# Squares of the keys issued a group later on ScalarE, and the keys' transposes in a PSUM bank of their own

## The chip, the cores and the metric

The kernel runs on one core of a Trainium2 chip. The metric is the device time of one execution in microseconds (us), the median of the runs. Everything is in float32. Five engines work beside each other, each through its own instructions in order: TensorE (PE, with its weight loads as PEld), VectorE (DVE), ScalarE (ACT), GpSimd (POOL) and SyncE (SP), which here issues DMAs.

## The reference

Two layers run one after the other on eight sequences of 100 tokens (512 wide), with a context of 722 rows for each sequence. The first layer aligns tokens to context rows by dynamic time warping, sums for each token the context rows that are matched to it into the tokens, and then runs a mixture of 16 experts in which each token goes to three. The second layer is a cross-attention with normalised queries and keys, and a feed-forward part. What the change touches are the keys and values of that second cross-attention:

```python
xn = layernorm(x, ln_x_g, ln_x_b)            # x: the context rows
ln = layernorm(latents, ln_l_g, ln_l_b)      # latents: the tokens
q = ln @ W_q
kv = jnp.concatenate([xn @ W_kv, ln @ W_kv], axis=1)
k, v = (kv[..., :INNER], kv[..., INNER:])
...
qn = rmsnorm(q, q_gamma) * SCALE
kn = rmsnorm(k, k_gamma)                     # n = norm(k) / sqrt(64); k / max(n, 1e-8) * gamma, for each head
sim = jnp.einsum('bhid,bhjd->bhij', qn, kn)
```

The context's part of keys and values depends on nothing that the first layer computes, so it can be done at any time before the attention.

## The kernel before

The kernel is one program whose instruction order on each engine is fixed when it is built, by a scheduler that goes by priorities and by its own estimates of durations. So work of different stages stands interleaved in each queue, and since every engine takes its queue in order, an instruction that has to wait holds up everything behind it, of whatever stage.

The stages around the change, with the lines of the profile:

- *Alignment* (codes L369 to L376, wave L392 to L395, traceback L440 with one step a token): almost all on VectorE. It ends at 402.80 us, with the copy `sel` (L448) behind it.
- *Keys and values of the context*, called the key stage here (L678 to L769): runs beside the alignment on PE, ScalarE and GpSimd, and reaches on into all stages down to the first expert slot. It is the code that the change edits.
- *Sums*: path values are spread over partitions by PE (`pf`, L453), copied by ScalarE (`fb`, L458), turned into selections by VectorE (`below` and `on`, L469 and L470), multiplied with the context rows `cr` (DMAs L476 and L479) by PE (`pe`, L483), copied (`er`, L485), moved by DMA to `E` (L490), and added to the tokens X by VectorE (L494).
- *Routing*: normalised tokens `xh`, transposed on PE (`pt`, L550) and multiplied with the gate (`pl`, L554, its logits `g` read at L558); then softmax, ranks (`pw`, L571) and places on VectorE; `pg`/`gT` (L668, L669) and `po` (L673, added to X at L674) bring in the experts' second bias; 21 indirect DMAs on GpSimd put the tokens into their experts' rows (`xs_d`, L645).
- *Expert slots* (`slot`, L778): SP fetches an expert's weights `w1t`, `w2t`, its bias `b1t` and its rows `xr` (L785 to L792); PE transposes the rows (`px`, L796), VectorE copies them (`xe`, L798); then PE computes `ph` (L807) and `py` (L822). Weights of odd slots lie in a pool, `moewb`, that takes the memory which the key stage used, so they are fetched when the key stage's last use of it has ended.
- Then the attention, which reads keys and values back from the DRAM tensors `k_d` and `v_d`, and the feed-forward part.

The key stage handles 16 groups: for each of eight sequences, two groups of three chunks of 128 context rows. `products` does a group's matmuls and copies; `keys` normalises and transposes the keys of a group, and is called one group behind. In `products`, each chunk has two PSUM tiles, `pk` and `pv`, of four matmuls each (L720); ScalarE copies the key tile with its row scale (`k`, L724), GpSimd adds the bias (L725), ScalarE copies the value tile (`vr`, L726); after the three chunks GpSimd issues the values' DMAs to `v_d` (L728, L733). Then ScalarE takes the squares of each chunk and head (8 heads, so 24 a group, L737, with the sum into `rk`), and the root (L740). In `keys` VectorE takes maximum and reciprocal of `rk` (L746, L747), GpSimd multiplies the keys with it chunk by chunk (L750), PE transposes each chunk in four pieces (`ptk`, L754), ScalarE copies these out (`kt`, L755), and GpSimd issues the DMA to `k_d` (L757).

All PSUM tiles of the key stage share one pool with one tag, so `pk`, `pv` and `ptk` take turns in four banks. In SBUF `k`, `vr` and `rk` have two buffers each, and `kt` and the scratch `kjunk` one.

Of the kernel before, what the change touches and what calls it, by code (L numbers as in the profile page):

```python
# [1 line left out]

# [7 lines left out]
F32 = mybir.dt.float32  # L10
U8 = mybir.dt.uint8
I32 = mybir.dt.int32
AF = mybir.ActivationFunctionType
# [4 lines left out]
P = 128  # L18
B, S, D = 8, 100, 512
# [11 lines left out]
NH, DH = 8, 64  # L31
# [38 lines left out]
def kernel(  # L70
# [25 lines left out]
    nc = tc.nc  # L96
# [98 lines left out]
    def ranks(sc, ne, pool):  # L195

        tri = pool.tile([P, ne, ne], F32, tag="tri", name="tri")
        nc.gpsimd.memset(tri, 1.0)
        nc.gpsimd.affine_select(
            out=tri, in_=tri, compare_op=ALU.is_gt, fill=0.0, base=0,  # L200
            pattern=[[1, ne], [-1, ne]], channel_multiplier=0,
        )
        other = sc.unsqueeze(2).to_broadcast([P, NT, ne, ne])
        own = sc.unsqueeze(3).to_broadcast([P, NT, ne, ne])
        ahead = pool.tile([P, NT, ne, ne], F32, tag="ahead", name="ahead")
        same = pool.tile([P, NT, ne, ne], F32, tag="same", name="same")
        nc.vector.tensor_tensor(ahead, other, own, ALU.is_gt)
        nc.vector.tensor_tensor(same, other, own, ALU.is_equal)
        nc.vector.tensor_tensor(same, same, tri.unsqueeze(1).to_broadcast([P, NT, ne, ne]), ALU.mult)
        nc.vector.tensor_tensor(ahead, ahead, same, ALU.add)  # L210
        rank = pool.tile([P, NT, ne], F32, tag="rank", name="rank")
        nc.vector.tensor_reduce(rank, ahead, AX.X, ALU.add)
        return rank, tri
# [27 lines left out]
    with tc.tile_pool(name="dwork", bufs=2, side="right") as dw, tc.tile_pool(name="dpsum", bufs=6, space=PSUM) as dps:  # L241
# [9 lines left out]
        pb = dps.tile([P, D], F32, tag="mm", name="pb")  # L251
# [16 lines left out]
        for b in range(B):  # L268
# [25 lines left out]
            r0, c0 = LAG + b * LANES, (B - 1 - b) * GW  # L294
# [30 lines left out]
    kvp = kv_scope.enter_context(tc.tile_pool(name="kv", bufs=2, side="right"))  # L325
    kps = kv_scope.enter_context(tc.tile_pool(name="kvpsum", bufs=4, space=PSUM, side="right"))
# [5 lines left out]
    with tc.tile_pool(name="align", bufs=2) as al:  # L332
# [77 lines left out]
        k, i = 1, 0  # L410
        while k < LANES:
            nc.vector.stream_shuffle(moved[:, body], last[:, i, LEAD - k : LEAD - k + NSTEP], over(k))
            nc.vector.tensor_tensor(last[:, 1 - i, body], last[:, i, body], moved[:, body], ALU.max)
            k, i = 2 * k, 1 - i
# [15 lines left out]
        for j in range(S - 1, -1, -1):  # L430
# [8 lines left out]
            junk = al.tile([B, W], F32, tag="junk", name="junk", bufs=1)  # L439
# [6 lines left out]
    with tc.tile_pool(name="sums", bufs=2) as sp, tc.tile_pool(name="spsum", bufs=4, space=PSUM) as sps:  # L446
# [4 lines left out]
        for b in range(B):  # L451
            k = b % half
# [49 lines left out]
    if True:  # L502
# [176 lines left out]
        mean = kvw.tile([P, P], F32, name="mean")  # L679
        nc.gpsimd.memset(mean, 1.0 / D)  # L680
        for half, dst in ((0, kbias), (1, vbias)):
            pb = kps.tile([P, D], F32, tag="mm", name="kvb")
            for dc in range(DC):
                nc.tensor.matmul(
                    pb, lncol[:, 1, dc : dc + 1].to_broadcast([P, P]), wc[:, dc, half * D : (half + 1) * D],
                    start=dc == 0, stop=dc == DC - 1,
                )
            nc.scalar.copy(dst, pb)
        pb = kps.tile([P, D], F32, tag="mm", name="kvc")
        for vc in range(DC):  # L690
            for dc in range(DC):
                nc.tensor.matmul(
# [5 lines left out]
            nc.scalar.mul(wc[:, dc, :], wc[:, dc, :], lncol[:, 0, dc : dc + 1])  # L698
        cm = kvw.tile([P, 2 * D], F32, name="cm")
        for half in range(2):  # L700
            pb = kps.tile([P, D], F32, tag="mm", name="kvm")
            for dc in range(DC):
                nc.tensor.matmul(
                    pb, mean, wc[:, dc, half * D : (half + 1) * D], start=dc == 0, stop=dc == DC - 1
                )
            nc.scalar.copy(cm[:, half * D : (half + 1) * D], pb)
        for dc in range(DC):
            nc.gpsimd.tensor_tensor(wc[:, dc, :], wc[:, dc, :], cm, ALU.subtract)
        def products(b, ct, c0):

            k = kvp.tile([P, 3, D], F32, tag="k", name="k")
            vr = kvp.tile([P, 3, D], F32, tag="vr", name="vr")
            rk = kvp.tile([P, 3, NH], F32, tag="rk", name="rk")
            for c in range(c0, c0 + 3):
                rs = crstd[:, b, c : c + 1]
                pk = kps.tile([P, D], F32, tag="mm", name="pk")
                pv = kps.tile([P, D], F32, tag="mm", name="pv")
                for ps, lo in ((pk, 0), (pv, D)):
                    for dc in range(DC):
                        nc.tensor.matmul(  # L720
                            ps, ct[:, dc, c * P : (c + 1) * P], wc[:, dc, lo : lo + D], start=dc == 0, stop=dc == DC - 1
                        )
                kc = k[:, c - c0, :]
                nc.scalar.mul(kc, pk, rs)  # L724
                nc.gpsimd.tensor_tensor(kc, kc, kbias, ALU.add)  # L725
                nc.scalar.mul(vr[:, c - c0, :], pv, rs)  # L726
            full = 3 if c0 == 0 else 2
            nc.gpsimd.dma_start(  # L728
                out=v_d[b, c0 * P : (c0 + full) * P, :].rearrange("(c p) d -> p c d", p=P), in_=vr[:, :full, :]
            )  # L730
            if c0 > 0:
                for r0, r1 in ((0, RLAST // 16 * 16), (RLAST // 16 * 16, RLAST)):
                    nc.gpsimd.dma_start(out=v_d[b, (RC - 1) * P + r0 : (RC - 1) * P + r1, :], in_=vr[r0:r1, 2, :])  # L733
            junk = kvp.tile([P, DH], F32, tag="kjunk", name="kjunk", bufs=1)
            for c in range(3):
                for h in range(NH):
                    nc.scalar.activation(  # L737
                        junk, k[:, c, h * DH : (h + 1) * DH], AF.Square, accum_out=rk[:, c, h : h + 1]
                    )
            nc.scalar.activation(rk, rk, AF.Sqrt, scale=1.0 / DH)  # L740
            return b, c0, k, rk

        def keys(b, c0, k, rk):

            kt = kvp.tile([P, NPAIR, 3 * P], F32, tag="kt", name="kt", bufs=1)
            nc.vector.tensor_scalar_max(rk, rk, 1e-8)  # L746
            nc.vector.reciprocal(rk, rk)  # L747
            for c in range(3):
                kh = k[:, c, :].rearrange("p (h d) -> p h d", h=NH)
                nc.gpsimd.tensor_tensor(kh, kh, rk[:, c, :].unsqueeze(2).to_broadcast([P, NH, DH]), ALU.mult)  # L750
                ptk = kps.tile([P, D], F32, tag="mm", name="ptk")
                ptv = ptk.rearrange("p (c n) -> p c n", c=NPAIR)
                for hp in range(NPAIR):
                    nc.tensor.transpose(ptv[:, hp, :], k[:, c, hp * P : (hp + 1) * P], ident)  # L754
                nc.scalar.activation(kt[:, :, c * P : (c + 1) * P], ptv, AF.Copy, scale=gcol[:, 1:2])  # L755
            w = min(S2 - c0 * P, 3 * P)
            nc.gpsimd.dma_start(out=k_d[b, :, :, c0 * P : c0 * P + w], in_=kt[:, :, :w])  # L757

        behind = None
        for b in range(B):  # L760
            ct = kvp.tile([P, DC, RC * P], F32, tag="ctk", name="ctk")
            nc.gpsimd.memset(ct[:, :, S2:], 0.0)
            nc.gpsimd.dma_start(out=ct[:, :, :S2], in_=context_t[b].rearrange("(c p) i -> p c i", p=P))
            for c0 in range(0, RC, 3):
                now = products(b, ct, c0)
                if behind is not None:
                    keys(*behind)
                behind = now
        keys(*behind)  # L769

        slots = moe.enter_context(ExitStack())
# [84 lines left out]
        with tc.If(some > 0):  # L856
            with tc.tile_pool(name="spw", bufs=1) as mw, tc.tile_pool(name="sph", bufs=2) as mh, tc.tile_pool(
                name="sppsum", bufs=4, space=PSUM
# [35 lines left out]
    if True:  # L894
# [8 lines left out]
        if True:  # L903
# [63 lines left out]
            with tc.tile_pool(name="qkv", bufs=2, side="right") as qp:  # L967
# [5 lines left out]
                for t in range(NT):  # L973
# [64 lines left out]
                    while r0 < t * P + n:  # L1038
                        b = r0 // S
# [6 lines left out]
                    while given < B and (given + 1) * S <= t * P + n:  # L1046
                        pv = aps.tile([P, D], F32, tag="po", name="apv", bufs=1)
# [5 lines left out]
                        vr = qp.tile([S, D], F32, tag="avr", name="avr")  # L1053
# [128 lines left out]
            def project(t):  # L1182
                n = tok_rows(t)
                py = aps.tile([P, D], F32, tag="tr", name="py", bufs=1)
                for dc in range(DC):
                    nc.tensor.matmul(  # L1186
                        py[:n], oT[:, dc, t * P : t * P + n], wo[:, dc, :], start=dc == 0, stop=dc == DC - 1
                    )
                return py
# [7 lines left out]
            done, ets, behind = 0, {}, None  # L1197
# [3 lines left out]
            with hand:  # L1201
                for g in range(B * NPAIR):
                    b, hp = g // NPAIR, g % NPAIR
# [8 lines left out]
                    if behind is not None and hp == 3:  # L1212
                        added(*behind)
                        behind = None
# [49 lines left out]
    with tc.tile_pool(name="ffn", bufs=1) as fp, tc.tile_pool(name="ffnt", bufs=3) as ft, tc.tile_pool(  # L1264
        name="fpsum", bufs=2, space=PSUM
# [48 lines left out]
        rank, _ = ranks(w, FE, fp)  # L1314
# [181 lines left out]
```

## Time and profile before

| | |
|---|---|
| median of the runs | 1538.27 us (three runs, 1536.83 to 1538.72) |
| the profiled execution | 1538.33 us |
| span of its trace | 1536.6 us |
| mean granted clock of TensorE | 0.949 |
| PE busy | 1385.6 us, 90% of the span |
| matmuls of pk and pv (L720) | 191.9 and 176.1 us |
| squares on ScalarE (L737) | 98.0 us, and 72.0 us of reading their sums |
| PE idle ahead of pk | 25.8 us, of which 22.7 for ScalarE's copy of vr |

Lines of the profile name the source line, the engine, the operation and its tiles (output<-inputs). Behind a bar stand busy time and the mean duration of one in ns, then the idle time of that engine just before such instructions, and what ended it. Waits are told as "engine, tile and line <- what it waited for: us in all, times, longest". The timeline shows start, duration and, in brackets, the idle time before. A clock of 0.50 in a window means that TensorE was granted half of its clock.

Some places of the trace that the prediction refers to: the sums' `pf` starts at 411.60 us; `pe` of the last sequence ends at 487.8; routing's last logits (`pl`) end at 529.5; the 21 puts lie between 561.63 and 588.3; the last `po` is at 608.30; the first slot's `px` starts at 613.63 and its `ph` at 616.88; the second slot's `ph` starts at 649.13.

### The profile page before, as it was taken

The page shows a single profiled execution, that of the slowest core. Times are in us where ns is not written, and L with a number is a line of the kernel's source. Part 1 is how long each engine was busy: PE and PEld are TensorE (multiplying, and loading weights), DVE is VectorE, ACT ScalarE, POOL GpSimd, SP SyncE. Part 2 cuts the span into 40 slices and gives each one's busy share as a digit, 9 for nine tenths or more (in the row PEclk, how much of TensorE's full clock was granted, in tenths as well). Part 3 has the DMA queues.
Part 4 walks back from the last instruction along what each step waited for, and adds up shares of the span by engine and source line. Part 5 has one row for each costly group of instructions (what it writes and reads, how often), then busy time and mean ns, then how long its engine had stood idle before and what let it go on. Part 6 is the DMA issues. An engine that isn't in the chain of part 4 may idle for free. (4 is left out here: it accounts for less than half of the span.)

```text
span 1536.6 us, 19541 instructions
## 1 busy us (share of the span) xinstructions
PE 1385.6 (90%) x7043; PEld 870.6 (57%) x7043; DVE 684.9 (45%) x1492; ACT 485.2 (32%) x1506; POOL 436.1 (28%) x552
## 2 busy tenths in 40 slices
PE   5979887989799998999999996499999997899998
PEld 4443333444333543899999995144476765544433
DVE  3579999799723251101100100634477773322220
ACT  3424354554522554121122221132354543200000
POOL 1014333545423356000000000600365554322210
PEclk8989899999999998899999998699899999999999
DMA  9861213542655143866567786521544420400000
GB/s 307 298 169 38 78 51 109 167 122 71 207 169 158 56 163 139 291 245 237 204 228 250 260 291 237 143 48 35 194 139 133 134 89 1 164 0 0 1 23 21
DMA packets 120857, 217.78 MB, mean 142 GB/s; under 512 B 47765, under 2 KB 49077, under 8 KB 120629
## 3 DMA queue, kind: packets, MB, share of 16 engines
q1 hardware_dynamic: 103413, 152.54, 30.9%
q0 software_dynamic: 16464, 61.44, 11.5%
q10 hardware_dynamic: 880, 2.51, 0.5%
q8 instruction: 58, 0.95, 0.3%
q14 instruction: 42, 0.34, 0.1%
HBM read 163.92 MB, written 50.86 MB: 140 GB/s over the span
## 5 line engine op out<-in xcount | busy, mean ns | idle before, releaser
L720 PE MATMUL pk<-wc,ctk 128*128 128x512 f32 x384 | 191.9, 641 | 25.8 <-ACT vr L726 22.7
L720 PE MATMUL pv<-wc,ctk 128*128 128x512 f32 x384 | 176.1, 597 | 0.0
L807 PE MATMUL ph<-xe,w1t 128*128 128x192 f32 (+4 forms) x1024 | 171.5, 314 | 1.3 <-DVE xe L798 1.3
L822 PE MATMUL py<-hT,w2t 128*128 128x192 f32 (+4 forms) x1024 | 169.7, 310 | 0.0
L807 PEld LDWEIGHTS ph<-xe,w1t 128*128 128x128 f32 x1024 | 154.4, 192 | 4.7 <-DVE xe L798 1.7
L822 PEld LDWEIGHTS py<-hT,w2t 128*128 128x128 f32 x1024 | 153.1, 191 | 1.8
L720 PEld LDWEIGHTS pk<-wc,ctk 128*128 128x128 f32 x384 | 76.9, 205 | 123.6 <-issue 92.8
L737 ACT ACTIVATE kjunk<-k 128x64 f32<-128x64 f32 x384 | 98.0, 255 | 111.3 <-POOL k L725 95.5
L811 ACT ACTIVATE hT<-ph,b1t 128x192 f32<-128x192 f32 (+4 forms) x128 | 51.8, 404 | 253.4 <-PE ph L807 253.4
L720 PEld LDWEIGHTS pv<-wc,ctk 128*128 128x128 f32 x384 | 73.1, 191 | 91.6 <-issue 88.6
L1129 ACT ACTIVATE et<-et,mk 128x200 f32<-128x200 f32 (+2 forms) x224 | 85.8, 451 | 67.2 <-DVE et L1123 67.1
L725 POOL TENSOR_TENSOR k<-k,kbias 128x512 f32<-128x512 f32 x48 | 71.9, 1503 | 99.1 <-ACT k L724 98.9
L798 DVE COPY xe<-px 128x768 f32<-128x768 f32 (+4 forms) x16 | 14.0, 875 | 185.8 <-PE ph L807 170.4
L835 POOL DMA_DIRECT2D ys_d<-yr x28 | 15.3, 547 | 285.8 <-ACT yr L834 285.8
L1356 PE MATMUL fpb<-xT,wi 128*128 128x400 f32 x256 | 91.5, 507 | 1.0 <-DVE z L1378 1.0
L1405 PE MATMUL fpo<-wot,hw 128*128 128x512 f32 x192 | 84.8, 595 | 0.0
L750 POOL TENSOR_TENSOR k<-k,rk 128x512 f32<-128x512 f32 x48 | 63.7, 1353 | 60.2 <-DVE rk L747 60.2
L440 DVE SCALAR_TENSOR_TENSOR junk<-two_i,path,C 8x735 f32<-8x735 f32 x64 | 74.1, 1157 | 9.7 <-DMA C<-step_d 7.7
L1113 PE MATMUL pst<-qt,akt 64*128 64x100 f32 x896 | 66.3, 282 | 6.8 <-DVE et L1123 6.7
L737 ACT ACTIVATION_READ_ACCUMULATOR kjunk<-k 128x1 f32 x384 | 72.0, 188 | 0.0
L1356 PEld LDWEIGHTS fpb<-xT,wi 128*128 128x128 f32 x256 | 47.0, 190 | 42.5 <-issue 9.4
L943 DVE CUSTOM_DVE_ANT_0 junk<-psc,mb 100x822 f32<-100x822 f32 x64 | 64.2, 1003 | 13.6 <-PE psc L933 13.3
(334 smaller groups left out, 2031.3 us busy)
## 6 DMA issues: line engine op xcount, KB each, us to landing
w1t<-in_w SPq DMA_DIRECT2D x16, 2048.0 KB
w2t<-in_w SPq DMA_DIRECT2D x16, 2048.0 KB
ct<-in_context_t SPq DMA_DIRECT2D x8, 1444.0 KB
ctk<-in_context_t POOLq DMA_DIRECT2D x8, 1444.0 KB
akt<-k_d SPq DMA_DIRECT2D x8, 1444.0 KB
cr<-in_context SPq DMA_DIRECT2D x8, 1280.0 KB
va<-v_d SPq DMA_DIRECT2D x8, 1280.0 KB
v_d<-vr POOLq DMA_DIRECT2D x8, 768.0 KB
```

The costliest lines, as they stand in the source:

```text
L440: nc.vector.scalar_tensor_tensor(junk, two_i1, path[:, j + 1 : j + 2], scol, ALU.is_le, ALU.mult, accum_out=path[:, j : j + 1])
L720: nc.tensor.matmul(ps, ct[:, dc, c * P : (c + 1) * P], wc[:, dc, lo : lo + D], start=dc == 0, stop=dc == DC - 1)
L725: nc.gpsimd.tensor_tensor(kc, kc, kbias, ALU.add)
L737: nc.scalar.activation(junk, k[:, c, h * DH : (h + 1) * DH], AF.Square, accum_out=rk[:, c, h : h + 1])
L750: nc.gpsimd.tensor_tensor(kh, kh, rk[:, c, :].unsqueeze(2).to_broadcast([P, NH, DH]), ALU.mult)
L807: nc.tensor.matmul(ph[:, :cap], st["w1t"][:, dc, hc * P : (hc + 1) * P], st["xe"][:, dc, :cap], start=dc == 0, stop=dc == DC - 1,)
L822: nc.tensor.matmul(py[:, dc, :cap], st["w2t"][:, hc, (2 * dh + dc) * P : (2 * dh + dc + 1) * P], st["hT"][:, hc, :cap], start=hc == 0, sto ...
L943: nc.vector.tensor_tensor_reduce(out=junk, in0=ps.rearrange("p b c -> p (b c)")[:S, :KEYS], in1=st["mb"], scale=1.0, scalar=-FMAX, op0=ALU ...
L1113: nc.tensor.matmul(ps[:, i, (c - c0) * S : (c - c0 + 1) * S], st["kt"][rows, hp, STARTS[c] : STARTS[c] + KP], qt[rows, hp, b * S : (b + 1) ...
L1129: nc.scalar.activation(et[:n, c - c0], et[:n, c - c0], AF.Exp, bias=mk[:n, b, c : c + 1])
L1356: nc.tensor.matmul(pb[:, :N2], wi[fc * P // FQ][:, dc, fc * P % FQ : fc * P % FQ + P], xT[:, dc, hh * N2 : (hh + 1) * N2], start=dc == 0, ...
L1405: nc.tensor.matmul(po[:n], hw[:, fc, t * P : t * P + n], wot[:, fc, :], start=fc == 0, stop=fc == FC - 1)
```

## The change

It has three parts. The squares and the root move from `products` into `keys`, and the squares of each chunk are put on ScalarE's queue behind the value copy of the same chunk of the following group, by an ordering edge (`tc.issue_after`) that adds no semaphore; for the last group there is no following group, and no edge. The transposes' tile `ptk` gets a tag of its own with one PSUM bank, and `pk`, `pv` and the setup's tiles keep three of the four. And `k` gets three buffers in place of two.

```diff
-                pk = kps.tile([P, D], F32, tag="mm", name="pk")
-                pv = kps.tile([P, D], F32, tag="mm", name="pv")
+                pk = kps.tile([P, D], F32, tag="mm", name="pk", bufs=3)
+                pv = kps.tile([P, D], F32, tag="mm", name="pv", bufs=3)
...
-            k = kvp.tile([P, 3, D], F32, tag="k", name="k")
+            k = kvp.tile([P, 3, D], F32, tag="k", name="k", bufs=3)
             vr = kvp.tile([P, 3, D], F32, tag="vr", name="vr")
-            rk = kvp.tile([P, 3, NH], F32, tag="rk", name="rk")
+            out_of = []
...
-                nc.scalar.mul(vr[:, c - c0, :], pv, rs)
+                out_of.append(nc.scalar.mul(vr[:, c - c0, :], pv, rs))
...
+            return b, c0, k, out_of
+
+        def keys(b, c0, k, _, later=()):
+
+            rk = kvp.tile([P, 3, NH], F32, tag="rk", name="rk")
             junk = kvp.tile([P, DH], F32, tag="kjunk", name="kjunk", bufs=1)
             for c in range(3):
-                for h in range(NH):
-                    nc.scalar.activation(
-                        junk, k[:, c, h * DH : (h + 1) * DH], AF.Square, accum_out=rk[:, c, h : h + 1]
-                    )
+                with tc.issue_after(later[c].ins) if later else nullcontext():
+                    for h in range(NH):
+                        nc.scalar.activation(
+                            junk, k[:, c, h * DH : (h + 1) * DH], AF.Square, accum_out=rk[:, c, h : h + 1]
+                        )
             nc.scalar.activation(rk, rk, AF.Sqrt, scale=1.0 / DH)
-            return b, c0, k, rk
-
-        def keys(b, c0, k, rk):
-
             kt = kvp.tile([P, NPAIR, 3 * P], F32, tag="kt", name="kt", bufs=1)
...
-                ptk = kps.tile([P, D], F32, tag="mm", name="ptk")
+                ptk = kps.tile([P, D], F32, tag="tk", name="ptk", bufs=1)
...
                 if behind is not None:
-                    keys(*behind)
+                    keys(*behind, later=now[-1])
                 behind = now
         keys(*behind)
```

More of the change, by code (lines that the diff above doesn't have):

```diff
@@ L1 @@
-from contextlib import ExitStack
+from contextlib import ExitStack, nullcontext
 import concourse.bass as bass
@@ L681 @@
         for half, dst in ((0, kbias), (1, vbias)):
-            pb = kps.tile([P, D], F32, tag="mm", name="kvb")
+            pb = kps.tile([P, D], F32, tag="mm", name="kvb", bufs=3)
             for dc in range(DC):
@@ L688 @@
             nc.scalar.copy(dst, pb)
-        pb = kps.tile([P, D], F32, tag="mm", name="kvc")
+        pb = kps.tile([P, D], F32, tag="mm", name="kvc", bufs=3)
         for vc in range(DC):
@@ L700 @@
         for half in range(2):
-            pb = kps.tile([P, D], F32, tag="mm", name="kvm")
+            pb = kps.tile([P, D], F32, tag="mm", name="kvm", bufs=3)
             for dc in range(DC):
```

## The prediction

> **What bounds the kernel now.** I read the page first (busy shares, then the costliest groups), then the waits of 120 to 630 us, the table of windows over the same time, and last the timeline at the places that these named. Groups of the page (busy time, mean of one, then idle time before them and what ended it), and three lines of the waits:
>
> ```profile
> PE 1385.6 (90%) x7043; PEld 870.6 (57%) x7043; DVE 684.9 (45%) x1492; ACT 485.2 (32%) x1506; POOL 436.1 (28%) x552
> ...
> L720 PE MATMUL pk<-wc,ctk 128*128 128x512 f32 x384 | 191.9, 641 | 25.8 <-ACT vr L726 22.7
> L737 ACT ACTIVATE kjunk<-k 128x64 f32<-128x64 f32 x384 | 98.0, 255 | 111.3 <-POOL k L725 95.5
> ```
> ```profile
> ACT kjunk L737 <- POOL k L725: 95.5, 39, 11.9
> ...
> DVE rk L746 <- ACT rk L740: 32.1, 5, 16.3
> ...
> PE ptk L754 <- ACT vr L726: 8.8, 4, 4.5
> ```
>
> TensorE is the busy engine, and the change aims at the few places where it isn't: it waits for ScalarE's copy of values (vr), which frees a PSUM bank. The timeline shows why that copy is late:
>
> ```profile
> 205.94 0.26 ACT L737 ACTIVATE kjunk<-k 128x64 f32<-128x64 f32 x1
> ...
> 206.57 0.67 ACT L726 ACTIVATE vr<-pv,crstd 128x512 f32<-128x512 f32 x1
> ...
> 207.29 6.41 PE L720 MATMUL pk<-wc,ctk 128*128 128x512 f32 x8 [3.10 <-ACT vr L726]
> ...
> 230.71 1.47 PE L754 MATMUL ptk<-ident,k 128*128 128x128 f32 x12
> 233.75 3.70 PE L720 MATMUL pk<-wc,ctk 128*128 128x512 f32 x8 [1.57 <-ACT vr L726]
> ```
>
> Squares wait for GpSimd's bias add and stand before the copy on the in-order ScalarE. Then 12 transposes take three of the four banks. The matmuls behind such a gap ran at half pace (6.41 us against 3.60). But to 402.8 us another engine sets the time beside this stage (windows; columns are busy us and count of PE, PEld, DVE, ACT, POOL, then granted clock):
>
> ```profile
> 200.00:300.00 100.00, 84.15 (x216) 38.82 (x215) 88.98 (x238) 50.32 (x213) 42.05 (x39) 0.93 0.38 124
> 300.00:400.00 100.00, 88.64 (x230) 41.09 (x229) 97.43 (x171) 53.30 (x231) 46.78 (x39) 0.95 0.36 106
> 400.00:450.00 50.00, 46.82 (x126) 21.06 (x125) 16.74 (x19) 19.98 (x80) 15.72 (x15) 0.97 0.52 166
> 530.00:562.00 32.00, 31.71 (x89) 14.88 (x88) 26.86 (x63) 20.27 (x79) 12.04 (x11) 1.00 0.21 71
> ```
>
> VectorE runs the alignment wave and its traceback, 97% busy up to the end at 402.8. What PE gains before that can only be kept as matmuls done early. From 402.8 the sequence is PE's: sums, routing, puts of the tokens, first expert slots, each with matmuls of the key stage standing between in a fixed order. The stage ends here:
>
> ```profile
> 627.17 1.84 ACT L755 ACTIVATE kt<-ptk,gcol 128x512 f32<-128x512 f32 x3
> ...
> 629.30 0.73 POOL L757 DMA_DIRECT2D k_d<-kt  x1 [17.10 <-ACT kt L755]
> ...
> 634.97 0.39 SPq L785 DMA_DIRECT2D w1t<-in_w  x1
> 634.98 0.31 POOL L902 MEMSET neg<- 100x256 f32 x1 [4.95 <-DMA k_d<-kt]
> ...
> 649.13 2.05 PE L807 MATMUL ph<-xe,w1t 128*128 128x224 f32 x10
> ```
>
> The second slot's weights (w1t at 634.97) go into memory of the key stage, so they wait for the last key DMA to land; from 649.13 PE is full to about 945 us. So the whole change is worth what it moves 649.13.
>
> **The change, part by part.** The profiled execution took 1538.33 us, span 1536.6, some 1.7 us outside; the median of the runs is 1538.27, so the sum is made against the median.
>
> *Squares moved.* Nothing is added or taken away: 24 squares a group at 0.38 us from one to the next (0.256 and the accumulator's read of 0.186, partly overlapped), so 3.05 us a chunk, still on ScalarE. ScalarE has about 15.3 us of work a group (six copies of 0.68, 24 squares, three kt copies, a root), PE 22.1 (24 matmuls at 0.858, transposes 1.5), so ScalarE stays under. What changes is lag: keys of group g are now ready only when all matmuls of group g+1 and 8 squares are done, one group later than before; its k*rk (GpSimd, 1.2 us each), transposes and kt follow in group g+2. No wait is added for GpSimd's bias, 95.5 us of ScalarE's waiting, and the copies pass the squares: the 22.7 and 8.8 us of PE's waits for vr go. Their cover for later lateness is k with three buffers instead of two, no time.
>
> *A bank of its own.* Transposes now stand a chunk (four) at a time among matmuls; each must wait until kt, 0.68 us, has emptied the single bank. In mid-stage 12 matmuls lie between: free. At the end of the stage, where nothing is left between them, it is one chunk after another: transposes 0.6, kt 0.68, three times about 1.4. With three banks for pk and pv, a copy of 0.69 us has two tiles (6.9 us) to come in: free also.
>
> *Wave phase: nothing gained.* VectorE is in order, and the changed kernel's instruction order puts each group's max and reciprocal (0.17 and 0.29 us) at a fixed place of the wave; by before's times these places lie 25 to 27 us apart (188.2, 214.6, 241.7, ... 396.8). PE needs 22.1 a group, so rk is ready before its place, and PE waits at the transposes instead of at vr. I take no stall of VectorE, and PE 7 us earlier at the sums (pf) because fewer matmuls stand ahead of it: 256 instead of 260 (3.4 us), 12 transposes fewer (1.5), and no group's gap of 2 to 4 us. Bounds: 0 if PE reaches there late anyhow; 11.6 if VectorE's last copy (done 404.54) did not hold it. The weights of the sums follow without a group's rk between them (0.5 us).
>
> *Sums to routing.* The sums' matmuls before batch 0 are in one stretch; I get pe finished at about 478 (was 487.8) and routing's last logits at 514 (was 529.5), of which 6 matmuls fewer in between are 5.2 us. This is a loan: those 6 and the earlier 4 come later.
>
> *Routing to the first slot*, counted from the last logits. Before pg/gT (pw in between) 25 matmuls stand where 18 did: +5, of which VectorE feels part. Three k*rk (3.1 us) stand on GpSimd directly before the 21 puts (1.29 us each), and VectorE's max and reciprocal of a group before the row of destinations; the puts start +38.7 us (before +32.1). The next key DMA stands behind the puts on GpSimd's queue and kt has one buffer: PE gets a gap of about 3.9 us. The first px comes at +85.2 (before +84.1), ph at +89.9 (before +87.4). The value DMAs (0.8 us each to issue) stay at the end of their group on GpSimd and wait for copies that now come earlier; SP's queue keeps the first slot's order, biases, rows, weights.
>
> *The tail, where it is given back.* At the first px before has all 192 transposes done but the last 12; the changed order has 32 left (rest of group 13, groups 14, 15), among px and ph of the first slot. For each group: three chunks 4.2 us, the key DMA from issue to landing 5.6 (629.30 to 634.93), since kt has one buffer. That is 9.9 a group, three times, from about +94: key DMAs land at about +104, +114, +124. py, behind the last transposes, starts at about +118 (before all py's first part had ended by +119.8), the weights of the second slot go out at +124.3 (before 634.97-529.5 = +105.5). ph of the second slot comes at +134 to +145, by how much of it runs at half clock, where before had +119.6: 648 to 659 against 649.1. Less about 1 us for transposes of a later slot already done: net -2 to +8; I take +4.5.
>
> Here a page of the Trainium skill decides the sign. The row says 5.6 us for the key DMA, at a DMA share of 0.67 in 630 to 635. "DMA: Bandwidth & Descriptors" (the table with the fixed cost) gives some 2.0 us fixed, to which its 676 KB come: at the 287 to 381 GB/s that the DMA view shows at 615 to 624 us, 1.8 to 2.4 us, so about 4.1 (an estimate from the page). By the page three landings are 4.5 us shorter, and the net is 0. I keep the row. On the other side, "TensorE: Matmul & The Clock Gate" (Why this matters) says one window of idleness, about 3 us, halves the clock. The trace agrees (0.50 from 608 to 621 after a gap of 2.96 and ones before), and the chain above makes three such gaps: a half-clocked stretch of 3.4 to 13.6 us, as the matmul durations show behind gaps, costs half its length; without the rule the tail is +134, with it +139.
>
> **Rivals.**
> 1. *The early gain survives* (faster): the tail's chain of transposes, kt and landings at 600 to 640 us runs beside ph and px of the first slot instead of ahead of py. It decides by when the last key DMA lands: from 627 us on down (514 + 113, a chain that starts as soon as px does and lands at the page's 4.1 us) the weights go out 8 us earlier than now, and with the puts' +6.6 also hidden all 15.5 us remain: 1523 to 1530. For it: 53.6 us of PE idleness lie in 118 to 613, and PE's work is unchanged. Against: one kt buffer, and weights that wait for the last landing.
> 2. *Slower, VectorE stalls in the wave*: rk now depends on the whole next group, and VectorE waits in order. Before, only the later rks made it wait (32.1 us, all after 402). Places 25 to 27 us apart leave 3 to 5 us a group over 22.1; the half clock after one gap (0.83 to 0.91 over 40 us windows) costs 3 to 7. It decides if a group takes over 27 us: then each of 9 places loses some 2 us, so +10 to +25: 1548 to 1563.
> 3. *The change moves nothing*: the waits change their names, the loan is paid back exactly: 1536 to 1540.
>
> **How the numbers follow.** A measurement of this kernel can tell about 0.2%, 3.1 us, from no change. Forecast (given back at the tail, 1536 to 1547, likeliest 1543): 0.45, of which slower 0.33, same 0.10, faster 0.02. Rival 1: 0.27, nearly all faster (0.26). Rival 2: 0.18, slower. Rival 3: 0.10, faster 0.02, same 0.04, slower 0.04. Sum: faster 0.30, same 0.15, slower 0.55. The range 1525 to 1560 leaves out parts of rivals 1 and 2; the forecast's own range is 1536 to 1547.
>
> **What would show it.** Right: waits of PE for vr gone in 120 to 400, waits of the transposes for k*rk in their place; end of the wave within 2 us of 402.8; last logits at 510 to 518; last key DMA landing at 634 to 642 and the second slot's ph at 648 to 659. Wrong: VectorE waiting for rk before 400 (rival 2), or the second slot's w1t issued before 630 (rival 1).

## The result, and the profile after

The changed kernel took 1544.73 us (median of five runs, 1543.83 to 1547.45) against 1538.27 for the kernel before: a ratio of 1.0045, 95% interval [1.0031, 1.0060], so 6.5 us slower; 1543.0 had been predicted. The profiled execution took 1543.83 us, its span is 1542.1. This result needs a caution that belongs beside it: the same kernel, run again in two later sets of runs, took 1535.92 and 1536.41 us, 0.9988 [0.9977, 1.0000] and 0.9992 [0.9978, 1.0006] of the kernel before. So the slowdown did not repeat; the experiments below show where those 8 to 9 us lie.

The same parts of the page as before: engines, the matmuls of pk, and the squares.

```profile
PE 1386.2 (90%) x7043; PEld 873.8 (57%) x7043; DVE 682.6 (44%) x1492; ACT 487.2 (32%) x1506; POOL 425.2 (28%) x552
...
L720 PE MATMUL pk<-wc,ctk 128*128 128x512 f32 x384 | 187.8, 631 | 3.1 <-POOL wc L708 3.1
...
L743 ACT ACTIVATE kjunk<-k 128x64 f32<-128x64 f32 x384 | 97.8, 255 | 10.8 <-ACT kjunk L743 1.0
```

The change did what it says: PE no longer waits for vr ahead of pk (22.7 us before, none now), and ScalarE's idle time ahead of squares fell from 111.3 us to 10.8. Yet PE is busy for the same 1386 us of a longer span. Its waits have only changed their names. From the waits of 120 to 400 us (engine, tile and line <- what it waited for: us, times, longest):

```profile
ACT kt L757 <- DMA k_d<-kt: 56.2, 7, 11.1
...
PE ptk L756 <- POOL k L752: 26.5, 6, 7.9
```

The transposes wait for keys that wait for VectorE's rk, and kt waits for the key DMA of the group before. The windows of the same stretches (columns as before):

```profile
200.00:300.00 100.00, 89.81 (x233) 41.84 (x233) 92.10 (x229) 51.56 (x219) 38.11 (x39) 0.93 0.38 125
300.00:400.00 100.00, 86.61 (x226) 39.80 (x224) 97.43 (x171) 54.21 (x228) 45.13 (x39) 0.96 0.34 99
400.00:450.00 50.00, 48.46 (x120) 22.27 (x121) 14.78 (x21) 14.35 (x58) 11.85 (x16) 0.91 0.72 222
530.00:562.00 32.00, 32.00 (x96) 15.33 (x95) 13.54 (x51) 18.31 (x83) 17.53 (x19) 1.00 0.44 162
```

And the end of the key stage, from the timeline:

```profile
631.60 0.69 ACT L757 ACTIVATE kt<-ptk,gcol 128x512 f32<-128x512 f32 x1 [5.40 <-DMA k_d<-kt]
...
632.43 1.09 PE L756 MATMUL ptk<-ident,k 128*128 128x128 f32 x4 [4.71 <-ACT kt L757]
...
636.25 16.54 PE L824 MATMUL py<-hT,w2t 128*128 128x256 f32 x64 [0.78 <-ACT kt L757]
636.49 0.72 POOL L759 DMA_DIRECT2D k_d<-kt  x1 [9.26 <-ACT kt L757]
640.73 0.39 SPq L787 DMA_DIRECT2D w1t<-in_w  x1
640.78 0.30 POOL L904 MEMSET neg<- 100x256 f32 x1 [3.57 <-DMA k_d<-kt]
...
652.63 1.68 PE L809 MATMUL ph<-xe,w1t 128*128 128x224 f32 x8
```

ScalarE stands 5.40 us for a landing, PE stands behind it, py comes at 636.25 (before 631.76), and the second slot's weights go out at 640.73 (before 634.97). The times at the marks of the prediction, in us from the start of the span; "again" is the second profile of the changed kernel, "kt2" the second profile of the version with two kt buffers:

| mark | before | changed | again | kt2 |
|---|---|---|---|---|
| pf starts | 411.6 | 400.2 | 400.8 | 400.5 |
| pe of the last sequence ends | 487.8 | 476.4 | 479.7 | 480.2 |
| last logits end | 529.5 | 513.0 | 516.3 | 517.7 |
| puts end | 588.3 | 575.5 | 578.9 | 579.9 |
| last po ends | 610.2 | 596.2 | 591.2 | 596.9 |
| first px | 613.6 | 602.6 | 597.4 | 601.4 |
| first py | 631.8 | 636.3 | 629.0 | 626.8 |
| second slot's w1t issued | 635.0 | 640.7 | 633.4 | 631.2 |
| second slot's ph | 649.1 | 652.6 | 645.1 | 641.1 |
| span ends | 1536.6 | 1542.1 | 1534.2 | 1528.4 |

### The profile page after: what moved, and what is told of

It reads as the page before. It is cut to its first block, busy times and chain, and to the rows that moved or that the text cites. A ratio compares the mean times of both kernels' runs of the same rounds, so it can differ in the third digit from the quotient of the medians.

```text
span 1542.1 us, 19576 instructions
## 1 busy us (share of the span) xinstructions
PE 1386.2 (90%) x7043; PEld 873.8 (57%) x7043; DVE 682.6 (44%) x1492; ACT 487.2 (32%) x1506; POOL 425.2 (28%) x552
## 3 DMA queue, kind: packets, MB, share of 16 engines
q10 hardware_dynamic: 880, 2.51, 0.5%
## 4 chain that ended last, share of the span: by engine, by line
PE 60%; DVE 16%; DMA 11%; issue 8%; ACT 2%; SPq 1%; POOL 1%; another core or an unknown queue 0%; POOLq 0%; DVEq 0%; ACTq 0%
PE py L824 10%; PE ph L809 9%; PE fpb L1358 6%; PE fpo L1407 5%; DMA cr<-in_context 4%; PE psc L935 3%; PE pst L1115 3%; DVE C L395 3%; PE pv L720 3%; PE pqk L1015 3%; PE pk L720 3%; DMA ct<-in_context_t 2%; PE apo L1143 2%; PE py L1188 2%; DVE best L394 2%
## 5 line engine op out<-in xcount | busy, mean ns | idle before, releaser
L720 PE MATMUL pk<-wc,ctk 128*128 128x512 f32 x384 | 187.8, 631 | 3.1 <-POOL wc L708 3.1
L743 ACT ACTIVATE kjunk<-k 128x64 f32<-128x64 f32 x384 | 97.8, 255 | 10.8 <-ACT kjunk L743 1.0
L752 POOL TENSOR_TENSOR k<-k,rk 128x512 f32<-128x512 f32 x48 | 58.6, 1248 | 121.6 <-DVE rk L749 103.1
L725 POOL TENSOR_TENSOR k<-k,kbias 128x512 f32<-128x512 f32 x48 | 68.0, 1445 | 79.1 <-ACT k L724 79.0
L440 DVE SCALAR_TENSOR_TENSOR junk<-two_i,path,C 8x735 f32<-8x735 f32 x64 | 77.4, 1210 | 6.8 <-DMA C<-step_d 4.8
L828 DVE COPY yT<-py 128x384 f32<-128x384 f32 (+4 forms) x32 | 16.5, 516 | 133.9 <-PE py L824 133.9
L1115 PEld LDWEIGHTS pst<-qt,akt 64*128 64x128 f32 x896 | 57.3, 191 | 27.7 <-DVE et L1125 18.6
```

Source lines behind the costliest of these rows:

```text
L440: nc.vector.scalar_tensor_tensor(junk, two_i1, path[:, j + 1 : j + 2], scol, ALU.is_le, ALU.mult, accum_out=path[:, j : j + 1])
L720: nc.tensor.matmul(ps, ct[:, dc, c * P : (c + 1) * P], wc[:, dc, lo : lo + D], start=dc == 0, stop=dc == DC - 1)
L743: nc.scalar.activation(junk, k[:, c, h * DH : (h + 1) * DH], AF.Square, accum_out=rk[:, c, h : h + 1])
L1115: nc.tensor.matmul(ps[:, i, (c - c0) * S : (c - c0 + 1) * S], st["kt"][rows, hp, STARTS[c] : STARTS[c] + KP], qt[rows, hp, b * S : (b + 1) ...
```

## The experiments

The theory: PE gains about 16 us up to the last logits, and the transposes that are left over give it back behind the first px, where each group's copies wait in one kt buffer for the landing of the key DMA before. The rivals: one of the two parts alone makes the effect; the tail is held by something else; or the loss lies elsewhere.

**Squares alone**: the changed kernel with its four banks shared again (pv and the setup's tiles likewise).

```diff
-                pk = kps.tile([P, D], F32, tag="mm", name="pk", bufs=3)
+                pk = kps.tile([P, D], F32, tag="mm", name="pk")
...
-                ptk = kps.tile([P, D], F32, tag="tk", name="ptk", bufs=1)
+                ptk = kps.tile([P, D], F32, tag="mm", name="ptk")
```

> Squares moved alone: keys of three buffers and the late squares as in the changed kernel, but transposes, pk and pv share four banks again. The instruction order that results has 192 pk/pv matmuls ahead of pf (changed kernel: 256) and 264 of 384 ahead of the first px. If the two parts carry each other (late keys need a bank that the following group's copies don't wait for): the 64 matmuls missing at pf are 55 us of PE time lost in the wave, so 1580 to 1600 us. If the late squares alone make the change's effect: 1541 to 1548 us, like the changed kernel.

Measured: 1652.91 us, ratio 1.0744 [1.0729, 1.0760]. The first branch had the sign right, and about half of the size. Waits of 120 to 400 us:

```profile
PE ptk L756 <- POOL k L752: 73.7, 13, 20.8
```

With shared banks nothing of the next group can be computed past a transpose that waits; late squares make that wait long (73.7 us by 400). And 120 of 384 matmuls (the profile counts each as two) were left for after the first px: py came at 745.8. Late squares need the bank.

**The bank alone**: the kernel before, squares in place, with the changed kernel's banks (pk, pv and the setup's tiles with three).

```diff
-                ptk = kps.tile([P, D], F32, tag="mm", name="ptk")
+                ptk = kps.tile([P, D], F32, tag="tk", name="ptk", bufs=1)
```

> The transposes' own bank alone, squares in place as before. By my theory the early gain comes from the late squares (PE no longer waits for vr) and the loss from the transposes left for the tail (24 of 192 stand behind the first px here, 32 in the changed kernel, 12 before): PE's waits for vr before 400 us stay, the last logits end within 5 us of 529.5, and the total is 1537 to 1543. If the one bank alone makes the loss by serialising transposes and copies: 1542 to 1550.

Measured: 1543.89 us, 1.0033 [1.0020, 1.0046], outside my theory's range and inside the other's. My step failed here: I had put the end of PE's waits for vr down to the squares. The bank alone ends them (22.7 to 0.4 us) and puts the same new wait in their place:

```profile
PE ptk L754 <- POOL k L750: 24.8, 8, 5.5
...
PE pk L720 <- ACT vr L726: 0.4, 2, 0.2
```

Squares still wait for the bias (85.6 us by 400), but PE's waits do not show it: pk and pv have three banks. The last logits ended at 523.2, so the bank alone brings 6.4 of the 16.6 us. At the second slot it is level with before (ph +0.5, then 0.8 us ahead up to the attention), the end of the span is +4.7: its loss lies in the attention, and is taken up below.

**Two kt buffers** (the setup's tile cm borrows a k buffer to make room).

```diff
-            kt = kvp.tile([P, NPAIR, 3 * P], F32, tag="kt", name="kt", bufs=1)
+            kt = kvp.tile([P, NPAIR, 3 * P], F32, tag="kt", name="kt")
```

> The changed kernel with two kt buffers (the setup's tile cm borrows a k buffer to make room). Theory (the early gain is given back in the tail because each group's copies wait for the landing of the key DMA before): ScalarE's waits of 62.7 us for k_d go, PE's gap of 4.71 us before the last transposes goes, the second slot's w1t is issued at 626 to 632 (changed kernel 640.7) and ph of the second slot at 638 to 646, total 1530 to 1537. Rival (the tail is held by the squares and the rk of the last groups on ScalarE, or by DMA traffic, not by kt): w1t at 638 or later, total within 3 us of 1544.7.

> Two kt buffers without the swap, once more. In its first profile ScalarE stood still for 9.9 us at 577 to 587. If that belongs to the build, it is there again and the total is 1541 to 1545; if not, it is 1532 to 1536, some 3 to 4 us above two kt buffers with bo ahead of mk (1530.3).

Measured: 1542.74 us the first time, 1.0026 [1.0013, 1.0038]; 1531.68 the second, 0.9957 [0.9941, 0.9973], beside the changed kernel's 1535.92 on the same chip. From the first px to the first py it took 24.3 and 25.4 us, where the changed kernel took 33.7 and 31.5. In the second profile none of the last copies waits for a landing:

```profile
623.79 0.69 ACT L757 ACTIVATE kt<-ptk,gcol 128x512 f32<-128x512 f32 x1
...
626.04 0.69 ACT L757 ACTIVATE kt<-ptk,gcol 128x512 f32<-128x512 f32 x1 [1.56 <-PE ptk L756]
...
626.78 14.08 PE L824 MATMUL py<-hT,w2t 128*128 128x256 f32 x64 [0.78 <-ACT kt L757]
```

Between px and py PE is idle for 1.9 us with two buffers and for 7.8 to 8.3 in the changed kernel's profiles, where one gap of 4.7 to 4.9 us stands behind the landing. So the single kt buffer does hold the end of the tail, as the theory has it. But not all of the 6 to 9 us are a gain: 24 transposes are left behind px in place of 32, since eight more stand ahead of it. Counted from the last logits, the second profiles have px 2.6 us later and py 3.5 us earlier with two buffers, and the total gained is 4.2 us. The first measurement spoke for the rival by its total and its w1t at 640.0, for a reason that the repeats below show.

**Maximum and reciprocal on GpSimd**.

```diff
-            nc.vector.tensor_scalar_max(rk, rk, 1e-8)
-            nc.vector.reciprocal(rk, rk)
+            nc.gpsimd.tensor_scalar_max(rk, rk, 1e-8)
+            nc.gpsimd.tensor_tensor(rk, rk, unit, ALU.pow)
```

(`unit` is a tile of -1.)

> The changed kernel with maximum and reciprocal of rk on GpSimd (maximum, then power -1) in place of VectorE. Theory (in the wave PE is held at the transposes by VectorE's fixed places, 31 us of gaps before 400): those gaps of PE go, but since the order still has pf behind 252 matmuls, PE waits at pf for the wave instead, in one gap of some 20 to 30 us; the wave ends 2 to 6 us earlier for the 0.46 us a group that VectorE no longer does, and that much is the gain: 1538 to 1544. Rival (the gaps are GpSimd's or ScalarE's own lateness): gaps before the transposes stay within a third of their sum, total 1543 to 1550.

Measured: 1560.22 us, 1.0145 [1.0130, 1.0160], above both ranges. The gaps went as expected, and came back as one, twice as long as I had put it:

```profile
347.26 0.60 PE L758 MATMUL ptk<-ident,k 128*128 128x128 f32 x4
402.38 3.73 PE L453 MATMUL pf<-path,sel 8*128 8x101 f32 x16 [54.51 <-DVE sel L448]
```

This shows two things. VectorE's fixed places do hold PE in the wave: without them PE is full from 200 to 348 us. And that is worth nothing, since 252 matmuls stand ahead of pf in the order whatever PE could do. The gain that I expected from a shorter wave did not come (it ended at 401.6; in the three profiles of the changed kernel at 398.7 to 399.3). The traceback, the last part of the alignment, began at 285.2 us instead of 273.7, behind a stretch in which GpSimd was busy for 46.6 of the 80 us from 120 on (changed kernel 28.9). And the tail got longer: group 13's key DMA went out at 631.6 (changed kernel 607.5), and from px to py it took 42.1 us.

**A pair of instructions in the attention.** In the profile the changed kernel was 2.1 us behind the kernel before from the second slot on (659 us), and lost 3.4 more in the attention, where its code is the same. There VectorE's order has two neighbours swapped: mk (which waits for the mask's DMA) ahead of bo. The timeline of the changed kernel:

```profile
1104.03 0.20 DVE L1093 TENSOR_SCALAR mk<-mt 128x64 f32<-128x64 uint8 x1 [8.64 <-DMA mt<-in_mask_t]
1104.14 0.68 DVE L1073 TENSOR_TENSOR bo<-bo,pbo 128x512 f32<-128x512 f32 x1
...
1104.91 8.61 POOL L1076 TENSOR_TENSOR X<-X,bo 128x512 f32<-128x512 f32 x7 [22.17 <-DVE bo L1073]
...
1120.79 0.56 PE L1169 MATMUL pws<-ws,ones 128*64 128x200 f32 x4 [2.90 <-POOL ws L1162]
```

and of the kernel before:

```profile
1098.25 0.69 DVE L1071 TENSOR_TENSOR bo<-bo,pbo 128x512 f32<-128x512 f32 x1 [7.30 <-PE pbo L1068]
1099.02 8.61 POOL L1074 TENSOR_TENSOR X<-X,bo 128x512 f32<-128x512 f32 x7 [20.73 <-DVE bo L1071]
1099.29 1.04 DVE L1091 TENSOR_SCALAR mk<-mt 128x64 f32<-128x64 uint8 x1 [0.35 <-DMA mt<-in_mask_t]
...
1114.93 0.56 PE L1167 MATMUL pws<-ws,ones 128*64 128x200 f32 x4 [2.51 <-POOL ws L1160]
```

From the first X add to pws it is 15.9 us in all: whatever delays bo delays PE. From the end of pbo to the first X add it is 0.8 us with bo first, and 5.4 here with mk first (1.0 to 5.4 in the kernels with that order). Four kernels swapped the pair, with this edit or, for the kernel before, its reverse:

```diff
-                nc.vector.tensor_tensor(bo, bo, pbo, ALU.add)
+                with_bias = nc.vector.tensor_tensor(bo, bo, pbo, ALU.add)
...
-            nc.vector.tensor_scalar(mk, ...)
+            with tc.issue_after(with_bias.ins):
+                nc.vector.tensor_scalar(mk, ...)
```

The changed kernel with bo first:

> The changed kernel with one instruction moved on VectorE: in the attention, bo<-bo,pbo stands ahead of mk<-mt as it does in the kernel before (all four changed kernels run so far have them the other way round; order on all other engines unchanged). Theory (3 of the 5.5 us of the changed kernel's profile are lost there: bo waits behind mk for the mask's DMA, GpSimd's seven X<-X,bo start later, the sums ws come later, PE's gap before pws reaches 3.4 us and the clock halves): GpSimd's X adds start by 3 to 5 us earlier, total 1539 to 1542. Rival (that loss is the clock's phase, which differs between executions of any kernel): total within 1.5 us of 1544.7.

The kernel before with mk first:

> The kernel before with the same two instructions the other way round: bo behind mk (one pair of GpSimd's adds for the sums changes places with it, all other orders unchanged). Theory: X adds start about 1.2 us later, PE's gap before pws grows from 2.5 to about 4, total 1540 to 1545. Rival: within 1.5 us of 1538.3.

Two kt buffers with bo first:

> The changed kernel with two kt buffers and bo ahead of mk. If both losses are as I read them (tail through the single kt buffer, attention through the swapped pair): about 2 us for kt as measured, 3 to 6 for the pair, 1536 to 1540, level with the kernel before. If the pair is nothing: 1542 to 1544, as with two buffers alone.

The bank alone with bo first:

> The transposes' own bank alone, with bo ahead of mk. The profile with the bank alone was 0.8 us ahead of before up to the attention and 4.6 behind at the end. Theory: the whole loss is the pair, so 1536.5 to 1540. Rival: 1542 to 1545.

Measured: 1536.07 us (0.9985 [0.9976, 0.9993]); 1541.16 (1.0015 [1.0008, 1.0022]); 1530.30 (0.9944 [0.9931, 0.9957]); 1542.46 (1.0026 [1.0015, 1.0036]). Only the second came as the theory has it: swapping the pair in the kernel before costs 2.3 us by the ratio. The first and third fell by 8.7 and 12.4 us against the kernels that they were made from, below both of their ranges and far more than the pair can give, and all of the surplus lay ahead of the attention, in instructions whose order was the same. That called for repeats.

The fourth went to the rival: with bo first the bank alone keeps its loss (1543.89 without). In its profile the first X add follows pbo by 0.8 us, and yet:

```profile
1115.80 0.94 PE L1168 MATMUL pws<-ws,ones 128*64 128x200 f32 x4 [4.00 <-POOL ws L1161]
```

PE had come to this place sooner (granted clock 1.00 from 1100 to 1110 us, in the kernel before 0.83), so it waited 4.00 us there instead of 2.51, and behind the gap it was granted half of its clock (0.50 from 1115 to 1124): it was 0.9 us behind the kernel before at pws and 4.0 at 1123. The same holds for all 14 profiles: in six the gap ahead of pws is 2.5 to 3.9 us and the four matmuls of pws take 0.56 us, in eight it is 4.0 to 4.3 and they take 0.93 to 0.94. Both kinds occur with bo first and with mk first. So the swap lengthens the gap, but the loss behind it is the clock's, and the bank alone pays it in either order; the changed kernel's first profile (2.90 us, 0.56) does not pay it, against what the first of the four expectations says, and loses by the late bo alone.

**The changed kernel again.**

> The changed kernel once more, to see what of its profile repeats. In the first profile ScalarE stood still twice (5.3 us ahead of a vr copy at 567.62, 5.7 ahead of the next at 579.18) and VectorE once (3.8 us ahead of an addition to X at 579.08) with no wait on data that explains it; the same instructions in the same order ran without these stops when bo stood ahead of mk, far behind them in the program. If the stops belong to the build: they are there again, po ends about 8 us later after the puts than with bo ahead, total 1543 to 1547. If they belong to one loading of the program or one chip: gone, and the total is 1538 to 1541, 3 us above bo ahead of mk.

> The changed kernel a third time: 1544.73 us in the first set of runs, 1535.92 in the second, each within 7 us of itself, while the kernel before gave 1538.1 to 1539.2 in all. If what differs is set once for a set of runs (a loading or a chip), this set lies again within a few us of one of the two, and its profile has the stops of ScalarE ahead of vr at about 562 us after the pattern (total above 1542) or has none (total below 1539). If it differs from execution to execution, the runs of this set spread over both.

Measured: 1535.92 and 1536.41 us, level with bo first (1536.07) and not 3 us above it. In both new profiles the stops (an engine standing still with its inputs complete) are gone. The first profile, in which the puts end at 575.5 us: the first copy's pv had been done for 5.2 us, the second copy waits for nothing that the trace shows, and VectorE stands as well (`remote` and `issue` stand where the profile finds nothing on this core that ended the wait):

```profile
558.79 3.60 PE L720 MATMUL pv<-wc,ctk 128*128 128x512 f32 x8
...
567.62 0.69 ACT L726 ACTIVATE vr<-pv,crstd 128x512 f32<-128x512 f32 x1 [7.87 <-PE pv L720]
...
579.18 0.69 ACT L726 ACTIVATE vr<-pv,crstd 128x512 f32<-128x512 f32 x1 [5.69 <-remote]
```
```profile
579.08 1.28 DVE L674 TENSOR_TENSOR X<-X,po 128x512 f32<-128x512 f32 x2 [3.83 <-remote]
...
579.82 3.78 PE L673 MATMUL po<-b2r,gT 16*128 16x512 f32 x4 [5.02 <-DVE X L674]
```

The same instructions in the second profile, whose marks up to the puts are 3.3 us later. Here each copy starts when its matmuls end, the second behind those at 572.69:

```profile
565.74 0.69 ACT L726 ACTIVATE vr<-pv,crstd 128x512 f32<-128x512 f32 x1 [2.67 <-PE pv L720]
...
574.72 0.69 ACT L726 ACTIVATE vr<-pv,crstd 128x512 f32<-128x512 f32 x1 [5.13 <-PE pv L720]
```
```profile
571.94 0.69 DVE L674 TENSOR_TENSOR X<-X,po 128x512 f32<-128x512 f32 x1 [1.45 <-PE po L673]
...
572.69 1.98 PE L720 MATMUL pv<-wc,ctk 128*128 128x512 f32 x4
```

Behind the late rk and its own stop VectorE's addition to X came 7.1 us later than in the second profile, PE stood 5.0 us for it at 574.8, and po ended 83.2 us after the last logits instead of 74.9. The order of instructions on every engine is the same in the three profiles. So those 8 us of the measured loss are stops, not the change's order of work. The kernel before had them too: its profile shows copies 2.1, 2.1 and 5.3 us late at 573 to 582,

```profile
572.98 0.69 ACT L755 ACTIVATE kt<-ptk,gcol 128x512 f32<-128x512 f32 x1 [2.15 <-remote]
...
582.20 0.69 ACT L726 ACTIVATE vr<-pv,crstd 128x512 f32<-128x512 f32 x1 [5.65 <-PE po L673]
589.62 0.26 ACT L737 ACTIVATE kjunk<-k 128x64 f32<-128x64 f32 x1 [6.73 <-issue]
```

while the kernel before with mk first, in a later set, has none of them and still comes to the same square no sooner than

```profile
589.06 0.26 ACT L737 ACTIVATE kjunk<-k 128x64 f32<-128x64 f32 x1 [11.88 <-POOL k L725]
```

There ScalarE had to wait for a bias add behind the puts in any case, and the stops lay under that wait. The bank alone, squares in place, shows it too: against its twin with bo first, ScalarE was 9.4 us behind by stops at a vr copy at 582.4 (measured from the last logits), and level again at the next square, at 584.7, which waited for the bias in both. The changed order took the squares out from behind the bias; the cover went with them. Stops of ScalarE or VectorE in this stretch are in all six profiles of the first two sets of runs (the two on record, squares alone, the bank alone, two kt buffers, GpSimd's maximum) and in none of the eight of the later sets. What they are is open. No wait on data in the trace accounts for them, and from 556 to 592 us of the first profile no instructions were fetched by DMA. One rival lies in the record and was not tested: the recording itself. The traces tell of landings by their semaphores; each of the eight profiles without stops holds 6803 such records, the six with stops 6428 to 6500. What is missing is missing here: from the first put to 5 us behind the last one there are 71 to 121 records with stops, and 352 to 384 without. Stops and missing records go together; which causes which, or whether a third thing causes both, no run here shows, since every time on record comes with a recorded span. Nor was it told apart whether the stops belong to a chip or to a loading of the program. Two of the 26 later executions of the changed kernel took 1544.6 and 1545.0 us; their traces are not kept, so stops in single executions are not excluded either.

**Squares of the last groups in place again**, on top of two kt buffers and bo first.

```diff
+            rk = squares(k) if 2 * b + c0 // 3 >= 10 else None
...
+            if rk is None:
+                rk = squares(k, later)
```

> Two kt buffers and bo ahead of mk, and groups 10 to 15 take their squares right behind their own copies again (16 transposes stand behind the first px instead of 24). Theory (the tail's chain of transposes, kt and landings sets py): py some 3 us earlier after px than with two kt buffers alone (25.0 us), total 1525 to 1530. Rival (the tail is now bounded by PE's own work or by the weights): within 1.5 us of 1530.3.

Measured: 1536.49 us, 0.9991 [0.9980, 1.0002], slower than without it (0.9944) and outside both ranges. From px to py it took 25.7 us, against 25.0 with two kt buffers and bo first, though eight transposes fewer were left, and px itself came 6.1 us later, behind transposes that waited for kt ahead of it (2.75 us at 596.7, 2.30 at 602.4). Fewer left-over transposes is not the point, then; where they wait seems to be, which this one run argues more than it shows.

The version that beats both kernels is two kt buffers on the changed kernel: 1530.30 us with bo first, 1531.68 without, where there are no stops (1542.74 with them). The two differ by 1.4 us on two chips, not by the 3 to 4 that I expected of the pair.

## Why the prediction was right, and where its steps were not

That 1544.73 lies within 2 us of 1543 is in part luck. The loan, and its repayment at the tail, are there as forecast. But stops of 8 us that nobody forecast made up for terms that were too large, and without them the changed kernel is not slower: 0.9988 and 0.9992, so the forecast sign rests on the stops.

- *Wave*: right that nothing is gained inside it for PE, that PE's waits move to the transposes, and against rival 2 that VectorE waits for no rk before 400 us (the first such wait is at 417.9). The wave itself ended 4.1 us earlier, which I had not expected; so pf gained 11.4 us, not 7. All of it lies ahead of the traceback, which began at 273.7 us instead of 278.7. The two profiles of the version with two kt buffers differ by 3.6 us in the same place, so how much of it is the change's is open. That the squares end the waits for vr was wrong: the bank does.
- *Sums to routing*: pe ended at 476.4 and the last logits at 513.0; I had 478 and 514. The loan is real: 16.6, 13.2 and 16.0 us in the three profiles.
- *Routing*: the first px came 89.6 us after the logits (predicted 85.2), ph 93.3 (89.9). Close, but for a wrong reason: I had a gap of 3.9 us at kt behind the puts. Without stops px came at 81.1 to 81.4, and that gap is 0.1 us or none. The term was 4 us too large; the stops filled it in the run on record.
- *Tail*: py at +123.3 (predicted +118), w1t at +127.7 (+124.3), ph of the second slot at +139.7 (+134 to +145), so +3.5 us where I took +4.5 with -2 to +8; the later slot's transposes gave back 1.4 (predicted 1). From px to py I had 32.8 us; it took 33.7, and 31.2 to 31.5 without stops. That sum held, but not by the chain that I gave for it, three groups of 9.9 us with a landing in each: only the last group's first copy stood long for a landing (5.40 us, and 1.12 for group 13's). Between the key DMAs of groups 13 and 14, at 607.5 and 626.5, PE is idle for 0.6 us: it has ph, px and transposes to do.
- *Without stops* py is at +112.6 to +112.7, w1t at +117.1 to +117.2, and ph of the second slot 4 to 7 us ahead of the kernel before, of which 1.2 to 1.8 us by the ratios are left in the total. So the loan is not quite paid back. The second slot's w1t goes out at 633.4 and 630.8, between the forecast and rival 1, and the totals lie where the forecast and rival 3 meet, 6 us above rival 1's.
- *The landing*: I kept the row's 5.6 us against 4.1, an estimate from the fixed cost of about 2.0 us in the Trainium skill's page "DMA: Bandwidth & Descriptors" (Anatomy of one DMA) and the measured bandwidth. The last landing, of the same 676 KB, took 4.3 us in the first two profiles (636.49 to 640.78 in the first), so there the estimate was nearer than the row. The one before, of 768 KB, took 5.1 and 5.3 (626.50 to 631.60, and 619.03 to 624.30). The term was over-sized by 1.3 us once, not by 4.5 in three landings.
- *The attention*: "the whole change is worth what it moves 649.13" failed. The order there was not the same, and 3.4 of the 5.5 us of span lie in it. Swapping the pair alone costs the kernel before 2.3 us; for the changed kernel 1536.07 with bo first stands against 1536.41 with mk first on the same chip, so no share of it in the total is shown there.
- *Smaller slips*: at the first px the kernel before has all transposes done, for its last twelve stand at 610.14, ahead of px. PE's idle time from 118 to 613 us is 51.8, not 53.6. And +139 less 1 gives +2.9 us, not the +4.5 that I took.

## What to carry to other kernels

Work that is done early on an engine with idle time is a loan if the order behind it is fixed: follow it to the last buffer that it must pass, here one kt tile and the landing of its DMA, before calling it a gain. A wait that is taken away may have covered another delay; look at what else that engine does in the stretch. Where a scheduler sets the order, compare it to the end of the program, also where no code was changed. And measure a small effect in more than one set of runs: the interval of one set tells nothing of what differs between sets.

## What the runs showed of the hardware that I had not expected

The changed kernel varied more between sets of runs (1535.92 to 1544.73 us) than the kernel before (1538.10 to 1539.23): one set of runs would have told 0.45% slower, another 0.1% faster. ScalarE stopped for 1.0 us between two squares of one tile (at 570.8 us in the first profile) and for 5.2 us ahead of a copy whose input was complete, both while GpSimd issued its 21 indirect DMAs.

Key DMAs of one size, 676 KB, took 7.6 us from issue to landing at 599.0 us and 4.1 at 626.4 in one profile (the changed kernel's third).

And a step of the traceback on VectorE (L440) took 1.0 us or 1.6 and more: in the changed kernel's first profile 26 of the 100 steps took 1.6 us or more, each with a GpSimd instruction beside it for at least three quarters of its time. In the version with maximum and reciprocal on GpSimd the last steps ran at 0.97 us beside a GpSimd that stood still. Other engines' work differs between these steps too, so this is an association and not a test.
